# A graph network's kernel: sixteen rows a step fetched by SyncE, and the two convolutions' ends rearranged

## The chip, the cores and the metric

The kernel runs on one core of a Trainium2 chip. Its engines each follow an instruction stream of their own and wait for one another through semaphores: PE (TensorE) multiplies matrices, DVE (VectorE) does elementwise work and reductions, ACT (ScalarE) does functions such as silu and sqrt, POOL (GpSimd) here issues the gathers of rows, and SP (SyncE) issues all other transfers. The metric is the device time of one execution in microseconds (us).

## The reference

A block of a graph network on N = 6,250 nodes with 128 features and 200,000 edges, which are sorted by their destination. Two mesh convolutions and one attention stage, each over all edges:

```python
h = relu(layernorm(x))
# mesh_conv, twice
m = concat([h[dst], h[src], edge_attr]) @ w1 + b1
m = silu(group_norm(m)) @ w2 + b2
h = segment_sum(m, dst) / max(count, 1)      # then group_norm, silu, and + time embedding / + x
# attention
logits = (q[dst] * k[src]).sum(-1) * scale + (edge_attr @ ew + eb)
w = segment_softmax(logits, dst)
o = segment_sum(w * v[src], dst) @ ow + ob
x = x + (h + group_norm(o))
```

The two halves of each `concat` are products per node, so they are made once per node and kept in tables in the chip's main memory: `a_d` (what an edge takes from its destination) and `b_d` (what it takes from its source); for attention `kv_d` holds k and v in rows of 256 numbers.

## The kernel before

**Tiles, chunks, windows.** The edges are cut into 1,563 tiles of 128, one edge per partition, and the tiles into 196 chunks of 8 (TPC; the last has 3). The nodes are cut into 49 windows of 128. A stage (conv 1, conv 2, attention as stage 3) walks over its chunks in `pipeline`, one step for each; the order of the instructions on DVE, ACT, PE and SP within a step is written out there and kept.

**A chunk of a convolution.** SP loads the destination rows `pk` (L724) and, every second step, numbers for the one-hot matrices `ohT` (L708, L711). POOL gathers the source rows into `g`, one instruction for each tile (L767), into a ring of buffers ahead of the use. ACT turns `ohT` into one-hot form (L733, L734). PE multiplies `ohT` with `pk` (L1227). DVE adds the product to `g` (L1234, "first"); ACT squares (L1236), DVE reduces (L1238), ACT takes the root (L1245), DVE the reciprocal, and three DVE operations of the whole chunk normalise (`normed`, L1249 to L1253). ACT applies silu (L1254), PE sums by destination (`summed`, L1259), ACT splits the sums by window (`by_window`, L1264) and DVE adds them to the nodes (`add_late`, L1269).

**Rows by SP.** For every eleventh chunk ("lone" chunks, 17 in a stage) POOL gathers only seven tiles. The eighth is fetched by SP, which loads twelve row numbers into its registers in each step (L689), works out an address for each, and issues a transfer of one row into `row_g` (L693); after eleven steps the 128 rows are there, and ACT copies them into `g` (L700). The class `Rows` does this; `by_rows` lists the chunks.

**Node work.** Once the edges of four windows are all summed, their node work is done beside the chunks, a piece in each step: a *batch* (`conv_nodes`, L1008 to L1074), whose products give the next stage's tables and whose copies (`n_o`, L1067, or additions L1065) are then stored. `plan_batches` lists the steps at which batches start: 14 in a convolution, at 81, 89 and so on to 185. A batch waits some idle steps before its silu (`n_t`, L966), the last one none. The nine windows that remain are done after the pipeline by `last_nodes`, with the tiles of its own pool. Before it every engine passes a barrier.

**Between the stages.** `last_nodes` stores the last rows of the tables, and the next stage's first gather waits for these stores. In the memory on the chip the tiles of `last_nodes` after conv 2 lie where stage 3 has its buffers `g`.

The functions that the change touches:

Of the kernel before, what the change touches and what calls it, by code (L numbers as in the profile page):

```python
# [10 lines left out]
I32 = mybir.dt.int32  # L11
AF = mybir.ActivationFunctionType
# [19 lines left out]
BN = 4  # L32
LG = 2
# [4 lines left out]
ROWS = 12  # L38
# [13 lines left out]
def kernel(ctx: ExitStack, tc: tile.TileContext, x, src, dst, eat, w, out):  # L52
# [607 lines left out]
    class Rows:  # L660


        def __init__(self, pool, table_d, width):
            self.pool, self.table_d, self.width = pool, table_d, width
            self.chunks, self.span = by_rows()
            self.starts = {c - 2 - self.span: c for c in self.chunks}
            self.now, self.got = None, {}
            self.at = {}
            if self.chunks:
                self.list_of(self.chunks[0])  # L670

        def list_of(self, c):
# [3 lines left out]
            self.at[c] = t  # L676

        def step(self, n):
            if n in self.starts:
# [6 lines left out]
            if self.now:  # L686
# [3 lines left out]
                    self.at[c][0:1, e:e + m], engines=[SP], min_val=0, max_val=N - 1,  # L690
                    skip_runtime_bounds_check_because="a source node")
                for j, a in enumerate(at):
                    nc.sync.dma_start(out=t[e + j:e + j + 1, :], in_=self.table_d[bass.ds(a, 1), :self.width])  # L693
# [252 lines left out]
    class Nodes:  # L946
# [14 lines left out]
        def turned(self, t, m, tag="x", silu=None):  # L961
# [3 lines left out]
            if silu:  # L965
                nc.scalar.activation(out, tp, AF.Silu, bias=cols[f"{silu}_b"], scale=cols[f"{silu}_g"])  # L966
            else:
                nc.scalar.copy(out, tp)
# [33 lines left out]
    def conv_nodes(b, i, w, m, idle=0, last=False):  # L1002
# [26 lines left out]
        if i == 1 or last:  # L1029
# [5 lines left out]
            tT = b.turned(A, m, "t", silu=f"n{i}")  # L1035
# [21 lines left out]
        for rhs, bias, d_ in ends:  # L1057
            o = b.times(tT, m, rhs)
            if bias:
# [97 lines left out]
    def last_nodes(i, hx=True):  # L1157

        with tc.tile_pool(name="lastn", bufs=1) as lp, tc.tile_pool(name="lastp", bufs=6, space=PSUM) as ps:
# [28 lines left out]
    def conv(i):  # L1188
# [6 lines left out]
        with ExitStack() as es:  # L1195
# [52 lines left out]
            def normed(k):  # L1248
                nc.vector.tensor_tensor(  # L1249
                    k.mt.rearrange("p t (g c) -> p t g c", c=HD), k.mt.rearrange("p t (g c) -> p t g c", c=HD),  # L1250
                    k.rs.rearrange("p (t g) -> p t g", g=H)[:, :, :, None].to_broadcast([P, k.nt, H, HD]), ALU.mult)
                nc.vector.tensor_tensor(k.mt, k.mt, over_edges(gam, k.nt), ALU.mult)  # L1252
                nc.vector.tensor_tensor(k.mt, k.mt, over_edges(bet, k.nt), ALU.add)  # L1253
                nc.scalar.activation(k.mt, k.mt, AF.Silu)  # L1254
# [16 lines left out]
            class Stage:  # L1271
# [38 lines left out]
                def second(self, run, ks, first):  # L1310
# [3 lines left out]
                    for k in ks:  # L1314
# [3 lines left out]
                        if k.c >= NCH - SOON and self.sums:  # L1318
# [4 lines left out]
                        normed(k)  # L1323
# [33 lines left out]
            stage.rows = Rows(rw, b_d[i], D)  # L1357
# [46 lines left out]
    with ExitStack() as es:  # L1404
# [168 lines left out]
        class Stage:  # L1573
# [4 lines left out]
            def __init__(self, bp):  # L1578
                self.bp = bp
                self.rows = Rows(rw, kv_d, KV)  # L1580
# [200 lines left out]
```

## Time and profile before

| what | before |
|---|---|
| median of 3 runs | 6,077.24 us (6,076.54 to 6,078.74) |
| profiled execution, its own time | 6,073.33 us |
| profiled execution, span | 6,071.6 us |
| gathers, conv 1 | 1,546, first at 56.23 us, last ends at 1,995.11 |
| gathers, conv 2 | 1,546, first at 2,059.76 us, last ends at 3,995.26 |
| gathers, stage 3 | 1,546, first at 4,049.09 us, the last near 5,991 |
| busy share of the span | DVE 82%, POOL 73%, PE 59%, PEld 56%, ACT 55% |

The span is what the profiler recorded of one execution. A row of a timeline reads: start, duration, engine, line of the kernel, operation, output and input tiles, and in brackets the idle time of the engine before it and what ended it. A row of groups gives busy time and mean duration in ns after the bar, and the idle time before with its releaser after the second bar. An engine with a q (SPq) is that engine's instruction queue, which issues transfers.

### The profile page before, as it was taken

The numbers are of one execution on the slowest core, as the hardware profiler recorded it, in microseconds if no ns is written. First come the engines' busy times: TensorE is split into PE (matmuls) and PEld (weight loads), VectorE is DVE, ScalarE is ACT, GpSimd is POOL, SyncE is SP. The second block draws the span as 40 slices with busy tenths as digits, with TensorE's granted clock in tenths as the row PEclk, the third lists the DMA queues.
The fourth block names the chain that finished last, engine by engine and source line by source line (L and its number), as shares of the span: only waits on it lengthen the run. The fifth ranks groups of instructions, "written<-read, shape, count | busy, mean of one in ns | idle before, by whom it ended". The sixth has DMA issues, their size and how long they took to land. (4 is left out here: it accounts for less than half of the span.)

```text
span 6071.6 us, 88562 instructions
## 1 busy us (share of the span) xinstructions
PE 3607.7 (59%) x20941; PEld 3418.2 (56%) x20942; DVE 4995.9 (82%) x7118; ACT 3351.4 (55%) x5310; POOL 4446.9 (73%) x4687
## 2 busy tenths in 40 slices
PE   5565556556556555555666666655666665566665
PEld 4555555555556455555555655554555555565554
DVE  7888888888888588878888888865788888888888
ACT  5666666666666566666666666642333333333354
POOL 5777777777777477777777777757777777777775
PEclk8777777777777677777778777776777777777787
DMA  5454343444444343443444444435566666656663
GB/s 159 116 133 120 100 112 101 109 109 104 109 104 111 75 103 97 102 103 100 104 114 115 110 115 111 116 104 155 159 162 165 167 165 166 168 159 168 164 166 85
DMA packets 409874, 760.21 MB, mean 125 GB/s; under 512 B 102703, under 2 KB 276530, under 8 KB 379937
## 3 DMA queue, kind: packets, MB, share of 16 engines
q0 software_dynamic: 173152, 405.57, 26.4%
q1 hardware_dynamic: 230544, 345.24, 21.0%
q10 hardware_dynamic: 5632, 3.50, 0.2%
q8 instruction: 173, 2.83, 0.2%
q14 instruction: 373, 3.06, 0.2%
HBM read 707.36 MB, written 46.58 MB: 124 GB/s over the span
## 5 line engine op out<-in xcount | busy, mean ns | idle before, releaser
L767 POOL DMA_INDIRECT g<-b_d,src_i x3092 | 2931.6, 948 | 954.3 <-issue 904.4
L1259 PE MATMUL u<-h,oh 128*128 128x129 f32 (+1 forms) x6252 | 1265.1, 384 | 1388.4 <-ACT h L1254 1388.2
L1259 PEld LDWEIGHTS u<-h,oh 128*128 128x128 f32 x6252 | 1167.1, 288 | 1469.8 <-ACT h L1254 1465.4
L767 POOL DMA_INDIRECT g<-kv_d,src_i x1546 | 1470.0, 951 | 490.6 <-issue 439.8
L1227 PE MATMUL m<-pk,ohT 101*128 101x128 f32 x6252 | 961.7, 319 | 193.1 <-DVE h L1234 151.7
L1227 PEld LDWEIGHTS m<-pk,ohT 101*128 101x128 f32 x6252 | 932.7, 236 | 210.3 <-DVE h L1234 166.9
L1234 DVE TENSOR_TENSOR h<-m,g 128x1024 f32<-128x1024 f32 x392 | 475.8, 1214 | 477.4 <-DMA g<-b_d,src_i 462.8
L1518 PE MATMUL us<-v,oh 128*128 128x145 f32 x3126 | 590.3, 357 | 378.3 <-DVE flat L1543 329.3
L1518 PEld LDWEIGHTS us<-v,oh 128*128 128x128 f32 x3126 | 545.2, 248 | 418.1 <-DVE flat L1543 241.8
L1438 PE MATMUL qe<-pk,ohT 101*128 101x136 f32 x3126 | 558.1, 348 | 335.0 <-ACT ebs L1455 319.1
L1438 PEld LDWEIGHTS qe<-pk,ohT 101*128 101x128 f32 x3126 | 518.6, 249 | 367.6 <-ACT ebs L1455 360.8
L1254 ACT ACTIVATE h<-h 128x1024 f32<-128x1024 f32 x392 | 412.9, 1053 | 544.5 <-DVE h L1253 527.9
L1236 ACT ACTIVATE sq<-h 128x1024 f32<-128x1024 f32 x392 | 411.8, 1051 | 486.3 <-DVE h L1234 484.1
L733 ACT ACTIVATE ohT<-ohT,minus_p 96x1024 f32<-96x1024 f32 x588 | 669.3, 1138 | 19.6 <-DMA ohT<-rel_d 19.5
L734 ACT ACTIVATE ohT<-ohT 96x1024 f32<-96x1024 f32 x588 | 619.9, 1054 | 18.7
L1238 DVE TENSOR_REDUCE var<-sq 128x64 f32<-128x1024 f32 x392 | 475.0, 1212 | 105.8 <-ACT sq L1236 105.0
L1252 DVE TENSOR_TENSOR h<-h,cps 128x1024 f32<-128x1024 f32 x392 | 477.1, 1217 | 13.5
L1253 DVE TENSOR_TENSOR h<-h,cps 128x1024 f32<-128x1024 f32 x392 | 477.0, 1217 | 13.4
L790 DVE TENSOR_TENSOR oh<-cps,dm 128x1024 f32<-128x1024 f32 x392 | 474.1, 1209 | 2.1 <-PE u L1259 2.1
L1249 DVE TENSOR_TENSOR h<-h,cps 128x1024 f32<-128x1024 f32 x392 | 473.9, 1209 | 0.0
L1453 DVE TENSOR_TENSOR g<-qe,g 128x768 f32<-128x768 f32 (+1 forms) x391 | 251.2, 683 | 211.2 <-DMA g<-kv_d,src_i 203.9
L1531 ACT ACTIVATE us<-d 128x16 f32<-128x16 f32 x196 | 36.6, 187 | 638.2 <-DVE d L1527 566.3
(288 smaller groups left out, 4271.9 us busy)
## 6 DMA issues: line engine op xcount, KB each, us to landing
ohT<-rel_d SPq DMA_DIRECT2D x291, 768.0 KB
row_g<-b_d SPq DMA_DIRECT2D x4352, 0.5 KB
g<-b_d,src_i POOLq DMA_INDIRECT x3092
row_g<-kv_d SPq DMA_DIRECT2D x2176, 1.0 KB
pk<-a_d SPq DMA_DIRECT2D x588, 46.0 KB
g<-kv_d,src_i POOLq DMA_INDIRECT x1546, 3.1
ohT<-in_eat_dram SPq DMA_DIRECT2D x291, 40.0 KB
a_d<-n_o SPq DMA_DIRECT2D x28, 256.0 KB
```

Of the source, the lines that this page charges most:

```text
L733: nc.scalar.activation(k.ohT[:WN, :], k.ohT[:WN, :], AF.Square, bias=minus_p[:WN])
L734: nc.scalar.activation(k.ohT[:WN, :], k.ohT[:WN, :], AF.Relu, bias=1.0, scale=-4.0)
L767: h = nc.gpsimd.indirect_dma_start(out=g[:, t, :table_d.shape[1]], out_offset=None, in_=table_d, in_offset=bass.IndirectOffsetOnAxis(ap=k. ...
L790: return nc.vector.tensor_tensor(k.oh[:, :k.nt, :], iota[:, None, :].to_broadcast([P, k.nt, P]), k.dm[:, :, None].to_broadcast([P, k.nt, P ...
L1227: nc.tensor.matmul(k.m[:, t, :], lhsT=lhs[:, t * P:(t + 1) * P], rhs=rhs, start=(j == 0), stop=(j == len(terms) - 1))
L1234: nc.vector.tensor_tensor(k.mt, k.m[:, :n], k.g[:, :n], ALU.add)
L1238: return lambda: nc.vector.tensor_reduce(var[:, at:at + n * H], sq[:, :n].rearrange("p t (g c) -> p (t g) c", c=HD), AX.X, ALU.add)
L1252: nc.vector.tensor_tensor(k.mt, k.mt, over_edges(gam, k.nt), ALU.mult)
L1253: nc.vector.tensor_tensor(k.mt, k.mt, over_edges(bet, k.nt), ALU.add)
L1259: nc.tensor.matmul(k.u[:, 0, :wide], lhsT=k.oh[:, t, :], rhs=k.h[:, t, :wide], start=(t == 0), stop=(t == k.nt - 1))
L1438: nc.tensor.matmul(k.qe[:, t // TB, at:at + DB], lhsT=lhs[:, t * P:(t + 1) * P], rhs=rhs, start=(j == 0), stop=(j == len(terms) - 1))
L1518: nc.tensor.matmul(k.u[:, :wide], lhsT=k.oh[:, t, :], rhs=k.v[:, t, :wide], start=(t == 0), stop=(t == k.nt - 1))
```

## The change

**Rows.** `ROWS` becomes 16: eight steps for a tile, every eighth chunk, 23 lone chunks in a stage instead of 17, at 13, 21 and so on to 189. DVE multiplies each list of row numbers by the row's length in bytes (`to_bytes`, 69 small instructions in the three stages, four steps after the list is requested). The table is seen as one run of bytes, so SP uses the number as an address. Fifteen of a step's sixteen transfers count up one of two semaphores of their own; only the sixteenth is tracked by the framework. ACT's copy waits for the count.

On SP, a step with rows in conv 1 before (`pk` is the load of destination rows, `row_at` the list of numbers); the pair of rows at the end goes on to twelve:

```order
L724 ISA
L724 DMA pk_662<-a_d_95 92x128
L689 TENSOR_LOAD row_at
L693 ISA
L693 DMA row_g<-b_d_98 1x128
```

and after:

```order
L748 ISA
L748 DMA pk_661<-a_d_95 92x128
L702 TENSOR_LOAD row_at
L708 DMA row_g<-b_d_98 1x512 x16
L748 ISA
L748 DMA pk_662<-a_d_95 92x128
L732 DMA ohT<-rel_d 96x2048
L735 DMA ohT<-in_eat_dram 5x2048
```

The arithmetic (ISA) ahead of each row is gone, and sixteen transfers stand in one run. POOL issues 1,540 gathers in each stage instead of 1,546.

**Batches of the convolutions.** They start at steps with remainder 5 by 8, at 85, 93 and so on to 181, and none in the last ten steps: 13 instead of 14. In conv 1 the last three have no idle steps, and with `fine` the last two spread a batch's transposes, silu, products and copies over more steps.

On ACT in conv 1, from the square of chunk 190 (`sq<-h_701`) on. Before, with a batch's copy (`n_o`), another's silu (`n_t`) and its table load ahead of the next compare (`ohT`):

```order
L1236 ACTIVATE sq<-h_701 128x1024
L1245 ACT_TABLE_LOAD
L1245 ACTIVATE sd<-var,eps_t 128x64
L1067 COPY n_o<-nd 128x512
L966 ACT_TABLE_LOAD
L966 ACTIVATE n_t<-nd,k_n_b,k_n_g 128x512
L733 ACTIVATE ohT<-ohT,minus_p 96x1024 x2
L734 ACTIVATE ohT<-ohT 96x1024
```

After:

```order
L1269 ACTIVATE sq<-h_701 128x1024
L1278 ACT_TABLE_LOAD
L1278 ACTIVATE sd<-var,eps_t 128x64
L757 ACTIVATE ohT<-ohT,minus_p 96x1024
L758 ACTIVATE ohT<-ohT 96x1024
L1301 ACTIVATE u<-u,mask 128x129 x2
L1291 ACT_TABLE_LOAD
L1291 ACTIVATE h_701<-h_701 128x8x128
L1269 ACTIVATE sq<-h_702 128x1024
L1278 ACT_TABLE_LOAD
L1278 ACTIVATE sd<-var,eps_t 128x64
L1096 COPY n_o<-nd 128x512
```

The last batch's silu now stands at step 188, one copy at step 190 ahead of these rows and the other at step 192, the last row shown. In conv 2 the last batch ends within the pipeline; before, its last addition (L1065, q) stood behind the pipeline's last sums.

**The last full chunk.** Chunk 194 is normalised in two halves of four tiles, and its sums are split by window only behind those of chunk 195. The last rows of ACT in a convolution's pipeline, before:

```order
L1264 ACTIVATE u<-u,mask 128x129 x2
L1254 ACT_TABLE_LOAD
L1254 ACTIVATE h_701<-h_701 128x8x128
L1264 ACTIVATE u<-u,mask 128x129 x2
L1254 ACTIVATE h_702<-h_702 128x3x128
```

and after:

```order
L1301 ACTIVATE u<-u,mask 128x129 x2
L1291 ACT_TABLE_LOAD
L1291 ACTIVATE h_701<-h_701 128x4x128 x2
L1291 ACTIVATE h_702<-h_702 128x3x128
L1301 ACTIVATE u<-u,mask 128x129 x4
```

The silu of chunk 194 became two, and the splits moved behind the silu of chunk 195.

**Between conv 2 and stage 3.** An unused tile of 50,528 bytes a partition ("below") moves the tiles of `last_nodes` up. They no longer lie under stage 3's `g`, but under its buffers `nbs`, `nbe`, `row_at` and the second `ohT`. The first gather of stage 3 waited for all eight lanes of SP's transfers before (stores of `kv_d`, `a_d` and `h_d`), and for six after (those of `kv_d`). On SP the loads of `row_at`, `nbs`, `nbe` and the first `ohT` now stand behind the `h_d` stores; before, they stood in conv 1's end.

The diff, at its core:

```diff
-ROWS = 12
+ROWS = 16
+BELOW = 12632
@@ plan_batches
-            if n % 8 == (4 if i == 3 else 1) and n > (40 if i == 3 else 80) and n + 6 < NCH \
+            if n % 8 == (4 if i == 3 else 5) and n > (40 if i == 3 else 80) and n + (6 if i == 3 else 10) < NCH \
@@ class Rows
+            self.bytes_d = table_d.rearrange("n c -> (n c)").bitcast(U8)
+            self.landed = [[tc.alloc_semaphore(f"{name}{j}"), 0] for j in range(2)]
+        def to_bytes(self, t):
+            nc.vector.tensor_scalar(t, t, 4 * self.width, None, ALU.mult)
         def step(self, n):
+            self.fresh -= 1
+            if self.fresh == 0:
+                self.to_bytes(self.at[max(self.at)])
...
                 for j, a in enumerate(at):
-                    nc.sync.dma_start(out=t[e + j:e + j + 1, :], in_=self.table_d[bass.ds(a, 1), :self.width])
+                    h = nc.sync.dma_start(out=t[e + j:e + j + 1, :].bitcast(U8),
+                                          in_=self.bytes_d[bass.ds(a, 4 * self.width)][None, :])
+                    if j == m - 1:
+                        tc.declare_fence(h.ins, group=key)
+                        continue
+                    tc.no_tile_sem_insts.add(h.ins.name)
+                    h.then_inc(s[0], 16)
+                    s[1] += 16
+                    tc.add_to_no_dep_group(key, h.ins)
...
-                nc.scalar.copy(k.g[:, TPC - 1, :self.width], self.got.pop(k.c))
+                s = self.landed[self.chunks.index(k.c) % 2]
+                nc.scalar.copy(k.g[:, TPC - 1, :self.width], self.got.pop(k.c)).wait_op(s[0], s[1], "sem-ge")
@@ conv_nodes
-            tT = b.turned(A, m, "t", silu=f"n{i}")
+            tp = b.in_bank(A, m)
+            if fine > 0:
+                yield
+            tT = b.silu_of(tp, m, f"n{i}")
...
-            if bias:
+            if bias or fine > 1:
                 yield
@@ last_nodes
+            if i == 2:
+                es.enter_context(tc.tile_pool(name="below", bufs=1)).tile([P, BELOW], FP, name="below")
@@ normed
-            def normed(k):
+            def normed(k, by=TPC):
+                for a in range(0, k.nt, by):
@@ second
-                        if k.c >= NCH - SOON and self.sums:
+                        if NCH - SOON <= k.c < NCH - 1 and self.sums:
...
-                        normed(k)
+                        normed(k, TPC // 2 if k.c == NCH - 2 else TPC)
@@ batch
-                    for r in conv_nodes(nodes, i, w, BN, idle=4 if j + 1 < len(plans[i]) else 0):
+                    for r in conv_nodes(nodes, i, w, BN, idle=4 if j + (3 if i == 1 else 1) < len(plans[i]) else 0,
+                                        fine=(j + 3 - len(plans[i])) * (i == 1)):
```

More of the change, by code (lines that the diff above doesn't have):

```diff
@@ L11 @@
 I32 = mybir.dt.int32
+U8 = mybir.dt.uint8
 AF = mybir.ActivationFunctionType
@@ L660, with __init__ @@
     class Rows:
[L663 to L664 removed]
+        def __init__(self, pool, table_d, width, name):
+            self.pool, self.table_d, self.width, self.name = pool, table_d, width, name
+            self.bytes_d = table_d.rearrange("n c -> (n c)").bitcast(U8)
             self.chunks, self.span = by_rows()
+            self.landed = [[tc.alloc_semaphore(f"{name}{j}"), 0] for j in range(2)]
             self.starts = {c - 2 - self.span: c for c in self.chunks}
@@ L670, in __init__ @@
                 self.list_of(self.chunks[0])
+                self.to_bytes(self.at[self.chunks[0]])
+                self.fresh = 0
         def list_of(self, c):
@@ L689, in step @@
                 _, at = nc.values_load_multi_w_load_instructions(
-                    self.at[c][0:1, e:e + m], engines=[SP], min_val=0, max_val=N - 1,
-                    skip_runtime_bounds_check_because="a source node")
+                    self.at[c][0:1, e:e + m], engines=[SP], min_val=0, max_val=(N - 1) * 4 * self.width,
+                    skip_runtime_bounds_check_because="where a source node's row begins")
+                s = self.landed[self.chunks.index(c) % 2]
+                key = f"{self.name}_{c}_{e}"
                 for j, a in enumerate(at):
-                    nc.sync.dma_start(out=t[e + j:e + j + 1, :], in_=self.table_d[bass.ds(a, 1), :self.width])
+                    h = nc.sync.dma_start(out=t[e + j:e + j + 1, :].bitcast(U8),
[7 more added lines that the diff above has]
+                    tc.add_to_no_dep_group(key, h.ins)
                 self.now[1] = e + m
@@ L959, in in_bank, with turned, silu_of @@
             return tp[:, :m, :]
-        def turned(self, t, m, tag="x", silu=None):
+        def turned(self, t, m, tag="x"):
             tp = self.in_bank(t, m)
             out = self.tile(m, tag)
[L965 to L968, printed above, removed]
+            nc.scalar.copy(out, tp)
+            return out
+        def silu_of(self, tp, m, n):
+            out = self.tile(m, "t")
+            nc.scalar.activation(out, tp, AF.Silu, bias=cols[f"{n}_b"], scale=cols[f"{n}_g"])
             return out
@@ L1000, in span, with conv_nodes @@
         return bass.ds(w, m) if not isinstance(w, int) else slice(w, w + m)
-    def conv_nodes(b, i, w, m, idle=0, last=False):
+    def conv_nodes(b, i, w, m, idle=0, last=False, fine=0):
         at = span(w, m)
@@ L1157, in last_nodes @@
     def last_nodes(i, hx=True):
-        with tc.tile_pool(name="lastn", bufs=1) as lp, tc.tile_pool(name="lastp", bufs=6, space=PSUM) as ps:
+        with ExitStack() as es:
+            if i == 2:
+                es.enter_context(tc.tile_pool(name="below", bufs=1)).tile([P, BELOW], FP, name="below")
+            lp = es.enter_context(tc.tile_pool(name="lastn", bufs=1))
+            ps = es.enter_context(tc.tile_pool(name="lastp", bufs=6, space=PSUM))
             n = NW - NWD
@@ L1246, in deviations @@
                 return sd
-            def normed(k):
[L1249 to L1254, printed above, removed]
+            def normed(k, by=TPC):
+                for a in range(0, k.nt, by):
+                    n = min(by, k.nt - a)
+                    mt = k.mt[:, a:a + n]
+                    m4 = mt.rearrange("p t (g c) -> p t g c", c=HD)
+                    nc.vector.tensor_tensor(
+                        m4, m4, k.rs.rearrange("p (t g) -> p t g", g=H)[:, a:a + n, :, None].to_broadcast(
+                            [P, n, H, HD]), ALU.mult)
+                    nc.vector.tensor_tensor(mt, mt, over_edges(gam, n), ALU.mult)
+                    nc.vector.tensor_tensor(mt, mt, over_edges(bet, n), ALU.add)
+                    nc.scalar.activation(mt, mt, AF.Silu)
             def summed(k):
@@ L1356, in conv @@
             stage = Stage()
-            stage.rows = Rows(rw, b_d[i], D)
+            stage.rows = Rows(rw, b_d[i], D, f"rows{i}")
             nodes.var = lambda: stage.var[:, NV:]
@@ L1579, in __init__ @@
                 self.bp = bp
-                self.rows = Rows(rw, kv_d, KV)
+                self.rows = Rows(rw, kv_d, KV, "rows3")
                 self.runs = list(steps_of(3)[0].values())
```

1 line of the change is left out of this document (added).

## The prediction

> **What bounds the kernel now.** I read the costliest groups first, then the waits, then the busy time of each stage's stretch of gathers, and last the timelines around the ends of the two convolutions. The page's chain of waits holds only shares of 0% and says nothing here.
>
> ```profile
> L767 POOL DMA_INDIRECT g<-b_d,src_i x3092 | 2931.6, 948 | 954.3 <-issue 904.4
> ...
> L767 POOL DMA_INDIRECT g<-kv_d,src_i x1546 | 1470.0, 951 | 490.6 <-issue 439.8
> ```
>
> ```profile
> POOL g L767 <- issue: 1344.2, 4409, 0.3
> ...
> DVE h L1234 <- DMA g<-b_d,src_i: 462.8, 166, 15.0
> ```
>
> ```profile
> core 0: us, PE busy (x) PEld busy (x) DVE busy (x) ACT busy (x) POOL busy (x), PEclk, DMA share, GB/s
> 56.00:1996.00 1940.00, 1144.99 (x6728) 1095.99 (x6726) 1610.21 (x1787) 1262.20 (x1558) 1467.15 (x1546) 0.75 0.44 112
> 2059.00:3996.00 1937.00, 1157.35 (x6756) 1105.44 (x6757) 1619.74 (x1663) 1251.99 (x1535) 1464.44 (x1546) 0.75 0.42 108
> 4049.00:5991.00 1942.00, 1184.46 (x6748) 1104.76 (x6748) 1594.07 (x3305) 740.91 (x2019) 1469.99 (x1546) 0.76 0.61 163
> ```
>
> Each stage issues 1,546 gathers. One keeps POOL busy 0.948 us and the next follows 0.30 us later, released by nothing but its own issue: a pitch of 1.25 us, 1,546 of which are the 1,937 to 1,942 us of each stretch. DVE is busy longer than POOL (1,610 us) but idles 17%, and in the convolutions its largest wait is for a gather. So POOL's sequence of gathers sets the pace, and the three stretches make 5,819 of the 6,071.6 us. The remainder lies around the stages' ends. At conv 1's end DVE's first operation on each of chunks 189 to 195 (L1234) stands so, with POOL's last gather ahead of it:
>
> ```profile
> 1994.17 0.94 POOL L767 DMA_INDIRECT g<-b_d,src_i  x1 [0.30 <-issue]
> ```
>
> ```profile
> 1947.07 1.22 DVE L1234 TENSOR_TENSOR h<-m,g 128x1024 f32<-128x1024 f32 x1
> ...
> 1966.48 1.22 DVE L1234 TENSOR_TENSOR h<-m,g 128x1024 f32<-128x1024 f32 x1
> ...
> 1977.63 1.22 DVE L1234 TENSOR_TENSOR h<-m,g 128x1024 f32<-128x1024 f32 x1
> ...
> 1993.19 1.22 DVE L1234 TENSOR_TENSOR h<-m,g 128x1024 f32<-128x1024 f32 x1
> ...
> 2005.23 1.22 DVE L1234 TENSOR_TENSOR h<-m,g 128x1024 f32<-128x1024 f32 x1
> ...
> 2017.63 1.22 DVE L1234 TENSOR_TENSOR h<-m,g 128x1024 f32<-128x1024 f32 x1
> ...
> 2021.11 0.55 DVE L1234 TENSOR_TENSOR h<-m,g 128x384 f32<-128x384 f32 x1
> ```
>
> The last gather ends at 1995.11 and the last chunk begins at 2021.11: DVE is 26.0 us behind. Chunk 189 was not: 42 gathers of 1.249 us follow its own (chunk 192 has 7, chunk 195 has 3), so its last ended at about 1942.65 and L1234 came 4.4 us later. The steps from chunk 189 to 194 took 19.4, 11.2, 15.6, 12.0 and 12.4 us, 70.6 in all, where their 39 gathers took 48.7. What makes them long is the node work of two batches, both still unfinished there. ACT, which goes strictly in order, stands 5.18 us before a batch's copy, and all later compares and square roots stand behind it:
>
> ```profile
> 2005.95 0.58 ACT L1067 COPY n_o<-nd 128x512 f32<-128x512 f32 x1 [5.18 <-PE nd L974]
> ```
>
> Conv 2, with one batch unfinished, loses less; the same rows for chunks 189, 190 and 192 to 195:
>
> ```profile
> 3994.32 0.94 POOL L767 DMA_INDIRECT g<-b_d,src_i  x1 [0.30 <-issue]
> ```
>
> ```profile
> 3943.98 1.23 DVE L1234 TENSOR_TENSOR h<-m,g 128x1024 f32<-128x1024 f32 x1
> ...
> 3961.70 1.22 DVE L1234 TENSOR_TENSOR h<-m,g 128x1024 f32<-128x1024 f32 x1
> ...
> 3981.30 1.22 DVE L1234 TENSOR_TENSOR h<-m,g 128x1024 f32<-128x1024 f32 x1
> ...
> 3989.79 1.22 DVE L1234 TENSOR_TENSOR h<-m,g 128x1024 f32<-128x1024 f32 x1
> ...
> 3998.53 1.22 DVE L1234 TENSOR_TENSOR h<-m,g 128x1024 f32<-128x1024 f32 x1
> ...
> 4002.60 0.55 DVE L1234 TENSOR_TENSOR h<-m,g 128x384 f32<-128x384 f32 x1
> ```
>
> One step of 17.7 us (the batch's silu), then undisturbed ones of 8.5 to 8.7: DVE catches up 1.3 us a chunk and ends 7.3 us behind the gather that ended at 3995.26.
>
> **Part 1, more rows by SP.** Six gathers fewer in each of three stages are 18 x 1.249 = **22.5 us**, if POOL still sets the pace. In stage 3 the last chunks run DVE-bound, but before and after alike two lone chunks lie there, so all six count. What it costs falls on SP, the DMA engines and DVE. SP's rows in one step before, in a convolution and in stage 3, and what one DMA and one load of row numbers take:
>
> ```profile
> 1015.24 5.12 SPq L693 DMA_DIRECT2D row_g<-b_d  x12
> ```
>
> ```profile
> 4910.59 7.84 SPq L693 DMA_DIRECT2D row_g<-kv_d  x12
> ...
> 4921.06 4.80 SPq L693 DMA_DIRECT2D row_g<-kv_d  x12
> ```
>
> ```profile
> L693 SPq DMA_DIRECT2D row_g<-b_d x4352: 224/228/1167, 95.1 to 3941.2; - x198
> ```
>
> ```profile
> L689 SPq TENSOR_LOAD <-row_at x561: 687/1007/2876, 93.9 to 5947.2; - x187
> ```
>
> Unhindered, twelve rows take 4.80 us, 0.40 each, of which the DMA is 0.228; the arithmetic between them goes. Sixteen then cost between 16 x 0.228 = 3.6 and 16 x 0.40 = 6.4 us. I take 0.30 a row, 4.8 us, nearer the lower end since the instruction that goes is the larger part of the difference. With 1.0 for the numbers' load and about 1.1 for the step's pk and ohT loads a step costs SP some 7 us (5.7 to 8.5), against 1,540 / 196 x 1.249 = 9.81 us of gathers. So it is hidden behind POOL, and only a row over (9.81 - 2.1) / 16 = 0.48 us would come through. The 7.84 us above shows that rows can be hindered (0.65 each): there a row waits for a semaphore lane that another load holds, and fifteen of sixteen rows no longer use one.
>
> The 2,304 rows more (69 x 128 less 51 x 128) load the DMA engines:
>
> ```profile
> q1 hardware_dynamic: 230544, 345.24, 21.0%
> ```
>
> 21.0% of 16 engines over 6,071.6 us, by 230,544 packets, is 0.0885 us a packet. The page counts 102,703 packets under 512 B, close to 6,528 rows x 16. So 36,864 more are 204 us for each of 16 engines, 3.4% of the span; the busiest stretch stands at 0.61 and goes to about 0.64. I count nothing, and at the other end 3.4% of stage 3's gathers' landing, which its 11 buffers cover. The Trainium skill speaks against it: "DMA: Bandwidth & Descriptors", section Specifications, wants at least 512 B for the line rate, and its section on semaphore increments splits one transfer over up to 16 engines. The trace agrees on the splitting; by that rule the rows are the dearest way to move these bytes, yet the sum stays, since engine time isn't what is short.
>
> The 69 multiplications of row numbers are small DVE instructions, priced by the nearest row:
>
> ```profile
> 2040.21 0.17 DVE L1008 TENSOR_SCALAR n_c<-flat 128x3 f32<-128x3 f32 x1 [2.33 <-DMA wcl<-wc_d]
> ```
>
> 69 x 0.17 = 12 us, 4 in each stage, inside DVE's 330 us of idleness in each: nothing, at most 12 if none were covered. The Trainium skill's "SBUF — State Buffer", section Who interferes with whom, has a tensor_scalar able to take the port that GpSimd shares, the other one blocking for the whole instruction. By that rule the sum would lose up to those same 12 us; the trace's gathers keep their 0.30 us gaps beside a DVE that is 83% busy.
>
> **Part 2, the batches earlier.** Conv 1's last two batches start at steps 173 and 181, not 177 and 185, and without idle steps; the earlier one is out of the tail, and the last has its silu at step 188 and two copies at 190 and 192. I charge the silu half of conv 2's excess of 7.7 us (its transposes are a step earlier now), each copy's step 2.2 us over ten (the 12.0 and 12.4 above), and give back 1.3 for each of three undisturbed ones: 4.4 + 3.9 + 4.4 - 3.9 = 8.8 us behind at the end, so 26.0 - 8.8 = **17 us**. Bounds: 21.6 if the tail ends as chunk 189 stood (4.4 behind), and 10 with both copies as dear as the 15.6 step. In conv 2 the silu also comes earlier: 2 us off the 7.3, between 0 and 4.
>
> **Part 3, the ends.** After the last chunk's first operation comes a fixed chain, up to the first gather of the next stage:
>
> ```profile
> 2037.45 0.42 DVE L1269 TENSOR_TENSOR flat<-flat,u 128x258 f32 x1 [2.48 <-ACT u L1264]
> ```
>
> ```profile
> 4018.34 0.68 DVE L1065 TENSOR_TENSOR n_o<-nd,r_qb 128x512 f32<-128x512 f32 x1
> 4022.72 0.31 DVE L1013 COPY n_c<-cnt 128x6 f32<-128x6 f32 x3 [3.70 <-SPq L799]
> ```
>
> ```profile
> L1015 DVE TENSOR_TENSOR n_x<-flat,n_c 128x512 f32<-128x512 f32 x28 | 19.4, 693 | 0.5
> ```
>
> Chunk 194 in halves starts its silu after three operations of 0.69 instead of 1.22 us, so 1.6 earlier, and products of chunk 195 and the window sums no longer wait in turn: about **3 us** of the 16.8 from 2021.11 to 2037.87 (between 0 and 4). Conv 2 has the same 3, and its last batch no longer runs past the pipeline: no addition at 4018.34 (0.7) and a barrier that need not wait for the batch's last store (3.70 against conv 1's 2.33, 1.3): **5 us**, between 2 and 6.
>
> ```profile
> 4036.95 4.94 SPq L1062 DMA_DIRECT2D kv_d<-n_o  x6
> ...
> 4044.01 1.80 SPq L1074 DMA_DIRECT2D h_d<-n_x  x3
> ```
>
> ```profile
> 4049.09 0.95 POOL L767 DMA_INDIRECT g<-kv_d,src_i  x1 [18.81 <-DMA ohT<-in_eat_dram]
> ```
>
> With the padded tile, stage 3's first gather waits for six lanes, those of the kv_d stores, not for eight. Their issue ends at 4041.89, the h_d stores' at 4045.81, 3.9 us later, and the gather started 3.3 after that. So **4 us**, 0 to 5. In exchange the nbs, nbe and first ohT loads are issued behind the h_d stores, on SP; chunk 0's compare is then late by a few us, with 11 chunks' worth of gather buffers to absorb it.
>
> Sum: 22.5 + 17 + 2 + 3 + 5 + 4 = **53.5 us**. The profiled execution took 6,073.33 by its own time, span 6,071.6 and 1.7 around it; that less 53.5 is 6,019.8. The median of the runs shown is 3.9 above the profiled one, so **6,024 us**.
>
> **Rivals.** *The tail stays long* (0.18): the copies wait for products that PE does in its own order, as the 5.18 us row shows, and two of them remain, so conv 1's steps stay near 12 to 15 us. Then its 17 and conv 2's 2 shrink to 3: 37.5 saved, 6,040. Against it: conv 2's undisturbed steps of 8.5. *Only the gathers count* (0.09): the ends turn out to be bound by PE's sums or by landing stores, and 22.5 is all: 6,055. *The rows take the gain back* (0.05): the 3.4% more engine time holds up the gathers' own transfers until POOL's gaps grow. A pitch of 1.258 instead of 1.249 (0.7%, a fifth of 3.4) on 4,620 gathers is 42 us: 6,066, within 0.2%. For: the gathers use the same 16 engines. Against: stage 3 at a share of 0.61 has the pitch of the convolutions at 0.44. *SP becomes the pace* (0.05, the other side): at L693 of the kernel before, the rows of one step. For: 7.84 us for twelve. From 0.48 us a row, SP's step is longer than the gathers', the copy out of row_g comes late, and POOL runs out of free g buffers. Each 0.01 us above costs 16 x 0.01 x 552 steps (23 chunks x 8 x 3) = 88 us; at 0.50 it is 177 less the 53 gained, 6,200. Against: unhindered it is 0.40 with the arithmetic that goes.
>
> **How the numbers follow.** The forecast has 0.63 and its own range 6,014 (every part at its better end, 63 us) to 6,036 (41 us; all at the worse end, 34.5, is less likely). The tail rival takes the range to 6,040, and 6,048 with some of the ends' terms lost besides; below it goes to 6,011, by the 2.2 us that the runs shown spread over. 6,011 to 6,048 leaves out the last three rivals. A change under 0.2% (12 us) can't be told from none here. Faster: 0.63 + 0.18 + 0.09 = 0.90; same 0.05; slower 0.05.
>
> **What would show it.** Right: 1,540 gathers a stage at an unchanged pitch of 1.25 us; row fetches x16 in about 5 us; L1234 of conv 1's chunk 195 about 9 us behind the last gather; 35.7 us rather than 38.7 from there to the next stage's first gather, and 37.5 rather than 46.5 at conv 2's end. Wrong: a row above 0.48 us, POOL waiting for a buffer, conv 1's steps after chunk 189 still 12 us or more, or gather gaps above 0.30 us beside the multiplications.

## The result, and the profile after

The changed kernel took a median of 6,022.5 us (four runs, 6,018.4 to 6,025.0) against 6,078.0 for the kernel before beside it; the ratio is 0.9907, with a 95% interval of 0.9890 to 0.9924. The forecast was 6,024 and its range 6,011 to 6,048. The profiled execution has a span of 6,016.3 us, 55.3 less than before. One set of the experiments ran on a chip on which SP was held up, where the kernel before took 8,584 us; it is compared with that time alone.

The groups and waits that answer to those shown of before, of the changed kernel (a gather is L791 now, DVE's first operation on a chunk L1267):

```profile
L791 POOL DMA_INDIRECT g<-b_d,src_i x3080 | 2921.7, 949 | 950.9 <-issue 903.8
...
L791 POOL DMA_INDIRECT g<-kv_d,src_i x1540 | 1464.4, 951 | 484.8 <-issue 433.4
```

```profile
POOL g L791 <- issue: 1337.2, 4386, 0.3
...
DVE h L1267 <- DMA g<-b_d,src_i: 444.4, 157, 14.7
```

POOL still waits for nothing but its own issue: 0.949 us and 0.30 behind it, as before, now 1,540 times a stage. Busy time in the three stretches of gathers:

```profile
56.00:1989.00 1933.00, 1128.99 (x6759) 1080.38 (x6757) 1623.85 (x1814) 1273.80 (x1574) 1462.52 (x1540) 0.76 0.44 112
2029.00:3957.00 1928.00, 1138.42 (x6736) 1086.18 (x6736) 1620.87 (x1675) 1253.55 (x1539) 1458.77 (x1540) 0.75 0.43 108
4000.00:5934.00 1934.00, 1169.24 (x6734) 1089.78 (x6735) 1598.53 (x3330) 745.61 (x2023) 1463.94 (x1540) 0.77 0.63 165
```

Conv 1's end, first POOL's last gather, then DVE's timeline: the first operations of chunks 189 to 195, DVE's last sum, and the first operation of the last nodes. The last row's bracket is the idle time before it:

```profile
1987.94 0.95 POOL L791 DMA_INDIRECT g<-b_d,src_i  x1 [0.30 <-issue]
```

```profile
1939.21 1.22 DVE L1267 TENSOR_TENSOR h<-m,g 128x1024 f32<-128x1024 f32 x1
...
1953.21 1.22 DVE L1267 TENSOR_TENSOR h<-m,g 128x1024 f32<-128x1024 f32 x1
...
1962.41 1.22 DVE L1267 TENSOR_TENSOR h<-m,g 128x1024 f32<-128x1024 f32 x1
...
1970.84 1.22 DVE L1267 TENSOR_TENSOR h<-m,g 128x1024 f32<-128x1024 f32 x1
...
1979.27 1.22 DVE L1267 TENSOR_TENSOR h<-m,g 128x1024 f32<-128x1024 f32 x1
...
1987.70 1.22 DVE L1267 TENSOR_TENSOR h<-m,g 128x1024 f32<-128x1024 f32 x1
...
1991.18 0.56 DVE L1267 TENSOR_TENSOR h<-m,g 128x384 f32<-128x384 f32 x1
...
2004.36 0.42 DVE L1306 TENSOR_TENSOR flat<-flat,u 128x258 f32 x1 [1.01 <-ACT u L1301]
...
2009.52 0.17 DVE L1034 TENSOR_SCALAR n_c<-flat 128x3 f32<-128x3 f32 x1 [4.73 <-issue]
```

The last gather ends at 1988.89 and chunk 195 begins 2.3 us later, where it was 26.0. One step, from chunk 189 to 190, still takes 14.0 us; the others take 8.4 to 9.2, and those of 8.4 catch up 1.5 us a chunk. The copies no longer make ACT wait; in the long step it waits for PE's sums:

```profile
1943.14 0.56 ACT L1096 COPY n_o<-nd 128x512 f32<-128x512 f32 x1
...
1953.17 0.72 ACT L1301 ACTIVATE u<-u,mask 128x129 f32<-128x129 f32 x2 [3.90 <-PE u L1296]
...
1966.29 0.57 ACT L1096 COPY n_o<-nd 128x512 f32<-128x512 f32 x1
```

That wait does not set the step's length. DVE is busy for 13.5 of the 14.0 us (the third pair of numbers below), for it normalises two chunks in this step (L1286 to L1290 run twice between two rows of L1267):

```profile
1939.21:1953.21 14.00, 7.64 (x48) 7.16 (x48) 13.49 (x16) 9.32 (x12) 10.60 (x12) 0.76 0.41 115
```

Conv 2's end on DVE (chunk 195's first operation, the last sum, the first operation of the last nodes), then POOL's last gather of conv 2 and stage 3's first:

```profile
3960.16 0.56 DVE L1267 TENSOR_TENSOR h<-m,g 128x384 f32<-128x384 f32 x1 [1.20 <-DMA g<-b_d,src_i]
...
3972.45 0.42 DVE L1306 TENSOR_TENSOR flat<-flat,u 128x256 f32 x1 [0.47 <-ACT u L1301]
3977.77 0.32 DVE L1039 COPY n_c<-cnt 128x6 f32<-128x6 f32 x3 [4.89 <-issue]
```

```profile
3956.51 0.94 POOL L791 DMA_INDIRECT g<-b_d,src_i  x1 [0.30 <-issue]
...
4000.39 0.95 POOL L791 DMA_INDIRECT g<-kv_d,src_i  x1 [15.08 <-ACT n_x L989]
```

Cut at these rows, the two profiled executions compare like this:

| piece of the span, us | before | after | saved |
|---|---|---|---|
| three stretches of gathers | 5,816.2 | 5,795.1 | 21.1 |
| conv 1: last gather's end to chunk 195's first operation | 26.0 | 2.3 | 23.7 |
| conv 1: from there to DVE's last sum | 16.8 | 13.6 | 3.2 |
| conv 1: from there to the last nodes' first operation | 2.3 | 4.7 | -2.4 |
| conv 2: last gather's end to chunk 195's first operation | 7.3 | 2.7 | 4.6 |
| conv 2: from there to DVE's last operation | 16.4 | 12.7 | 3.7 |
| conv 2: from there to the last nodes' first operation | 3.7 | 4.9 | -1.2 |
| conv 2: from there to stage 3's first gather | 26.4 | 22.6 | 3.8 |
| behind stage 3's last gather | 80.7 | 81.9 | -1.2 |

Together they are 55.3 us, with conv 1's last nodes at 19.5 us both times.

### The profile page after: what moved, and what is told of

Same layout as the page of the kernel before. It is cut to its first block, busy times and chain, and to the rows that moved or that the text cites. A ratio compares the mean times of both kernels' runs of the same rounds, so it can differ in the third digit from the quotient of the medians.

```text
span 6016.3 us, 86748 instructions
## 1 busy us (share of the span) xinstructions
PE 3547.9 (59%) x20869; PEld 3359.6 (56%) x20870; DVE 4994.1 (83%) x7165; ACT 3355.0 (56%) x5321; POOL 4431.3 (74%) x4669
## 3 DMA queue, kind: packets, MB, share of 16 engines
q1 hardware_dynamic: 234576, 345.26, 21.4%
## 5 line engine op out<-in xcount | busy, mean ns | idle before, releaser
L791 POOL DMA_INDIRECT g<-b_d,src_i x3080 | 2921.7, 949 | 950.9 <-issue 903.8
L1296 PE MATMUL u<-h,oh 128*128 128x129 f32 (+1 forms) x6252 | 1250.0, 381 | 1400.3 <-ACT h L1291 1400.2
L1296 PEld LDWEIGHTS u<-h,oh 128*128 128x128 f32 x6252 | 1153.9, 285 | 1481.1 <-ACT h L1291 1475.7
L791 POOL DMA_INDIRECT g<-kv_d,src_i x1540 | 1464.4, 951 | 484.8 <-issue 433.4
L1260 PE MATMUL m<-pk,ohT 101*128 101x128 f32 x6252 | 933.8, 313 | 179.4 <-DVE h L1267 134.0
L1260 PEld LDWEIGHTS m<-pk,ohT 101*128 101x128 f32 x6252 | 902.7, 229 | 197.2 <-DVE h L1267 150.2
L1267 DVE TENSOR_TENSOR h<-m,g 128x1024 f32<-128x1024 f32 x392 | 475.8, 1214 | 463.0 <-DMA g<-b_d,src_i 444.4
L1291 ACT ACTIVATE h<-h 128x1024 f32<-128x1024 f32 (+2 forms) x394 | 413.5, 1049 | 571.0 <-DVE h L1290 554.9
L1289 DVE TENSOR_TENSOR h<-h,cps 128x1024 f32<-128x1024 f32 (+2 forms) x394 | 477.5, 1212 | 13.5
L1290 DVE TENSOR_TENSOR h<-h,cps 128x1024 f32<-128x1024 f32 (+2 forms) x394 | 477.4, 1212 | 13.5
L1286 DVE TENSOR_TENSOR h<-h,cps 128x1024 f32<-128x1024 f32 (+2 forms) x394 | 474.1, 1203 | 0.0
```

Source lines behind the costliest of these rows:

```text
L791: h = nc.gpsimd.indirect_dma_start(out=g[:, t, :table_d.shape[1]], out_offset=None, in_=table_d, in_offset=bass.IndirectOffsetOnAxis(ap=k. ...
L1260: nc.tensor.matmul(k.m[:, t, :], lhsT=lhs[:, t * P:(t + 1) * P], rhs=rhs, start=(j == 0), stop=(j == len(terms) - 1))
L1267: nc.vector.tensor_tensor(k.mt, k.m[:, :n], k.g[:, :n], ALU.add)
L1289: nc.vector.tensor_tensor(mt, mt, over_edges(gam, n), ALU.mult)
L1290: nc.vector.tensor_tensor(mt, mt, over_edges(bet, n), ALU.add)
L1296: nc.tensor.matmul(k.u[:, 0, :wide], lhsT=k.oh[:, t, :], rhs=k.h[:, t, :wide], start=(t == 0), stop=(t == k.nt - 1))
```

## Experiments

Theory: POOL's gathers set the pace, SP's longer steps are hidden, and the batches' unfinished work was what made conv 1's tail long. Rivals: SP is near its limit; the tail had another cause; the rows and the ends don't add up.

**The rows alone, and the ends alone.**

```diff
# e1_rows_only: the kernel before with class Rows and its calls as changed
-ROWS = 12
+ROWS = 16
# e2_ends_only: the changed kernel with class Rows and its calls as before
-ROWS = 16
+ROWS = 12
```

> The kernel before with the rows' part alone: sixteen rows a step, byte addresses, own semaphores; batches, last chunk and memory of the ends as before. Theory (POOL's gathers set the pace, SP's longer steps are hidden): 18 gathers fewer, which the profile of after shows as 6 to 8 us in each stage, 21 in all, so about 6,057 us; conv 1's last chunk still begins 20 us or more behind its last gather. Rival (the rows by themselves cost what they save, and the ends made the whole gain): within 6 us of 6,078.

Measured: 6,057.4 us, ratio 0.9969 (0.9957 to 0.9980). Conv 1's lag stayed at 26.0 us, conv 2's at 7.3; the stretches of gathers were 1,933.0, 1,931.9 and 1,934.6 us.

> The changed kernel with the rows as before: twelve a step, SP's register arithmetic, tracked one by one, 1,546 gathers a stage; batches, halves and the tile below as changed. Theory (the parts add up): 6,022 plus the 21 us of 18 gathers, about 6,043; conv 1's last chunk begins 2 to 6 us behind its last gather, as in after. Rival (the short tail needs the rows' part, since before a lone chunk lay at 192 and SP was busier): a lag of 10 us or more in conv 1, and 6,052 or above.

Measured: 6,038.8 us, ratio 0.9939 (0.9923 to 0.9956), lags of 2.1 and 2.7 us. Against their runs of the kernel before (6,075.7) the rows save 18 us (12 to 26 by the interval) and the ends 37 (27 to 47), together 55, as the whole change does: as far as these intervals tell they add up, and neither needs the other.

**The batches as before.**

```diff
-            if n % 8 == (4 if i == 3 else 5) and ... and n + (6 if i == 3 else 10) < NCH \
+            if n % 8 == (4 if i == 3 else 1) and ... and n + 6 < NCH \
-                    for r in conv_nodes(..., idle=4 if j + (3 if i == 1 else 1) < len(plans[i]) else 0, fine=...):
+                    for r in conv_nodes(..., idle=4 if j + 1 < len(plans[i]) else 0):
```

> The changed kernel with the batches of the convolutions as before (14, at steps 81 to 185, idle steps in all but the last, none of the finer pieces); rows, halves and the tile below as changed. Theory (the batches' unfinished work makes the tail long): conv 1's last chunk begins 20 to 26 us behind its last gather and conv 2's 7, so some 21 + 4 us more than the changed kernel, about 6,048. Rival (the tail was long for another reason, such as the lone chunk at 192 or the last chunks' order): conv 1's lag stays under 10 us and the time within 6 of 6,022.

Measured: 6,044.5 us, 22 more than the changed kernel. Conv 1's lag is 19.3 us, just short of the 20 to 26 expected, conv 2's 7.3, and the copies wait again:

```profile
1951.05 0.59 ACT L1096 COPY n_o<-nd 128x512 f32<-128x512 f32 x1 [4.16 <-PE nd L1000]
...
1968.67 0.59 ACT L1096 COPY n_o<-nd 128x512 f32<-128x512 f32 x1 [3.74 <-PE nd L1000]
...
1981.83 0.59 ACT L1096 COPY n_o<-nd 128x512 f32<-128x512 f32 x1 [4.19 <-PE nd L1000]
...
1994.87 0.59 ACT L1096 COPY n_o<-nd 128x512 f32<-128x512 f32 x1 [4.75 <-PE nd L1000]
```

So the old batches are the cause of the long tail: with the same rows and halves, four copies fall into the tail and wait some 4 us each, 16.8 together, where the changed kernel has two copies that don't wait and a lag 17.0 us shorter. The run undoes the starts, the idle steps and the finer pieces together. That the finer pieces end the waits, because products that come a step after the silu are ready as ACT reaches the copy, is argued, not shown. Nor do the runs say what took the other 6.7 of conv 1's 23.7 us, for the rows alone left the lag at 26.0.

**The halves and the tile below, undone.**

```diff
-                        if NCH - SOON <= k.c < NCH - 1 and self.sums:
+                        if k.c >= NCH - SOON and self.sums:
-                        normed(k, TPC // 2 if k.c == NCH - 2 else TPC)
+                        normed(k)
-            if i == 2:
-                es.enter_context(tc.tile_pool(name="below", bufs=1)).tile([P, BELOW], FP, name="below")
```

> The changed kernel with two parts of the ends undone: chunk 194 normalised in one piece with its sums split where they were, and no tile that moves the last nodes' memory up before stage 3. Each is read at its own place in the trace. Theory: from the last chunk's first operation to DVE's last sum 16.8 and 16.4 us, as in the kernel before, not 13.6 and 12.7; and from the last nodes' first operation in conv 2 to stage 3's first gather 26.4, not 22.6 us. Some 10 us more than the changed kernel in all, less what the wait at the branch of L823 changes by. Rival for the tile below (the kv_d stores land last anyway, and the other stores cost nothing): 22.6 stays. Rival for the halves (the short tail of the batches alone brought the 3 us): 13.6 and 12.7 stay.

Measured, one run: 6,039.2 us, 17 more than the changed kernel where some 10 were expected. From chunk 195's first operation to DVE's last sum 16.8 us in conv 1 and 15.8 in conv 2 (16.4 before included a batch's addition); from the last nodes' first operation in conv 2 (3989.84) to stage 3's first gather 26.4 us:

```profile
4016.26 0.95 POOL L791 DMA_INDIRECT g<-kv_d,src_i  x1 [18.86 <-DMA pk<-a_d]
```

So both parts do what the forecast said: 3 us at each convolution's end, 3.8 before stage 3. Conv 1's lag was 6.4 us here, 4.1 more than with the halves. It opens at chunk 191, which neither part touches, where ACT waited for a load of `ohT` that came late:

```profile
1953.33 1.15 ACT L757 ACTIVATE ohT<-ohT,minus_p 96x1024 f32<-96x1024 f32 x1 [4.30 <-DMA ohT<-rel_d]
```

The changed kernel's profile has no such wait there; one run doesn't tell how often it comes.

**SP's budget: sixteen rows in the old way.**

```diff
 # the kernel before
-ROWS = 12
+ROWS = 16
```

> The kernel before with ROWS = 16 and nothing else: sixteen rows a step with SP's register arithmetic and with every row waiting for a lane. Theory of SP's pace: a row costs a mean of 0.50 us this way (5.8 us for twelve in the trace of before), so a step costs SP 16 x 0.50 + 1.2 + 1.1 = 10.3 us against 9.81 of gathers; 0.5 us more on some 184 steps in each stage, 270 us, less the 21 gained: about 6,330, and POOL waits for free buffers. Rival (the lane waits only fill SP's slack, and a row costs 0.40 where it matters): 8.7 us a step, hidden, 6,057 as with the byte addresses.

Measured: 6,424.1 us, ratio 1.0576 (1.0558 to 1.0594). This is the prediction's rival on the slower side, and it is what the rows would have cost without the byte addresses and own semaphores. A row cost 0.47 to 0.49 us on average. SP's waits for a free `ohT` buffer, which are its slack, show it best; before, after, and here:

```profile
SPq L708 <- PE m L1227: 526.1, 135, 12.9
...
SPq L708 <- PE qe L1438: 251.7, 50, 13.9
```

```profile
SPq L732 <- PE m L1260: 619.9, 160, 10.0
SPq L732 <- PE qe L1476: 366.3, 70, 17.2
```

```profile
SPq L708 <- PE m L1227: 47.8, 8, 13.2
SPq L708 <- PE qe L1438: 45.8, 4, 15.9
```

778 us of slack before, 986 after (with more rows), 94 here. With it gone ACT waits for loads (the wait of the first row below was 19.5 us before), and POOL for the chunks that should free its buffers:

```profile
ACT ohT L733 <- DMA ohT<-rel_d: 900.9, 186, 12.1
```

```profile
POOL g L767 <- DVE h L1234: 164.5, 91, 7.6
POOL g L767 <- DVE n_rs L1142: 162.4, 17, 11.2
```

The forecast for this run was 6,330, with 10.3 us a step; conv 1 took 2,043.5 us, 10.4 for each of its 196 chunks. Sixteen rows at 0.47 and 1.4 from the list's load to the first row leave about 1.4 us for the rest of a step, an estimate, where 1.1 was counted.

**Bytes, but every row tracked.** Here on an undisturbed chip; the same kernel on the other one is under "More rows".

```diff
-                    if j == m - 1:
-                        tc.declare_fence(h.ins, group=key)
-                        continue
-                    tc.no_tile_sem_insts.add(h.ins.name)
-                    h.then_inc(s[0], 16)
-                    s[1] += 16
-                    tc.add_to_no_dep_group(key, h.ins)
```

> The changed kernel with byte addresses but every row tracked, so that each of the sixteen waits for one of the eight lanes as before. Theory (of the 0.50 us a row before, 0.09 are lane waits: 588 us of them on 6,528 rows, and 0.08 the register arithmetic): 0.41 a row, 1.4 + 16 x 0.41 + 1.4 = 9.4 us a step, just hidden: 6,020 to 6,040. Rival (the lanes alone bring SP to its limit): 0.45 or more a row, a step above 9.9 us, 6,080 or more, with POOL waiting for buffers.

Measured: 6,043.8 us (two runs), ratio 0.9944 (0.9924 to 0.9964), 4 us above the range expected, with 0.41 us a row in conv 1 and 0.44 in stage 3. The convolutions' gathers are within 3 us of the changed kernel's (1,932.1 and 1,931.4 us), but stage 3's take 1,945.8 instead of 1,934.1 and its end 91.0 instead of 81.9. So of the old 0.50 us a row, 0.09 were arithmetic and 0.08 lane waits, and without the own semaphores SP's slack is down to 293 us:

```profile
SPq L705 <- DMA ohT<-rel_d: 603.0, 276, 4.6
SPq L721 <- PE m L1249: 229.7, 76, 10.7
...
SPq L721 <- PE qe L1465: 63.5, 9, 17.2
```

The first row is what rows waited for lanes; in the changed kernel it is gone. Roughly 20 us of the change's gain hang on the semaphores.

**More rows.** Four kernels ran on the chip with the held-up SP, whose single instructions were up to 1.4 us long there (source lines of `e9_shift88`; minimum, median and maximum in ns):

```profile
L708 SPq MOVE row_g<-b_d x5888: 1/29/1437, 121.3 to 5287.6; - x197
L708 SPq DMA_DIRECT2D row_g<-b_d x5888: 1/228/1424, 121.3 to 5287.6; - x197
```

Only places that SP doesn't reach are read from them.

```diff
-ROWS = 16
+ROWS = 19      # rows19; rows22: 22
```

> The changed kernel with ROWS = 19: seven steps for a tile, every seventh chunk, 27 lone chunks in a stage, four gathers fewer in each stage than the changed kernel. Theory (POOL's pace; SP's step of 1.4 for the list + 19 x 0.326 + 1.4 for the rest = 9.0 us stays under the 9.78 of the gathers): 12 gathers at the 1.16 us that each of the 18 brought so far, 14 us, about 6,008. Rival (the gain by gathers is used up, DVE or the batches set the pace from here): 6,018 to 6,026, and DVE no longer waits for gathers.

> The changed kernel with ROWS = 22: six steps for a tile, 31 lone chunks in a stage, eight gathers fewer in each. Theory of SP's pace: a step costs SP 1.4 + 22 x 0.326 + 1.4 = 10.0 us against 9.76 of gathers, so SP sets the pace by 0.2 us a step, some 45 us in each stage less 10 for the gathers: 6,100 or more, with ACT or PE waiting for loads and POOL for buffers. Rival (the other 1.4 us overlap or are rarer; SP stays hidden): 24 gathers x 1.16 = 28 us less than the changed kernel, 5,995.

> The changed kernel with byte addresses but every row tracked, so that each of the sixteen waits for one of the eight lanes as before. Theory (of the 0.50 us a row before, 0.09 were lane waits and 0.08 the register arithmetic): 0.41 a row, 16 x 0.41 + 2.8 = 9.4 us a step, just hidden: 6,020 to 6,035. Rival (the lanes are the larger part of what the change saves on SP): 0.45 or more a row, a step above 9.9 us, 6,100 or more.

Measured: ratios 1.1198 (1.1161 to 1.1236), 1.1771 (1.1741 to 1.1802) and 1.0022 (1.0001 to 1.0043). With SP as the bound, more rows simply cost more; the expectations, made for an undisturbed SP, can't be judged by these. So nineteen rows were repeated, with the 88 memsets of the next experiment:

> The changed kernel with ROWS = 19 (27 lone chunks in a stage, 12 gathers fewer in all) and the 88 memsets in conv 1 that move DVE's code. Theory: where SP is undisturbed a step costs it 1.4 + 19 x 0.326 + 1.4 = 9.0 us against 9.78 of gathers, so 12 x 1.16 = 14 us are gained; and the wait at the branch of L823 behind conv 1 is 0.5, not 2.9 us, likewise behind conv 2 if the place of the code decides it there too: 5 us; about 6,003 in all. Rival for the rows (SP is at its limit already): 6,030 or more, and POOL waits for buffers. Rival for the branch: 2.9 and 3.1 us stay, and the time is 6,008.

Measured: 6,617.5 us, ratio 1.0889 (1.0871 to 1.0907), where 6,003 was expected. The rows cost 0.326 us each, as in the changed kernel. SP's slack is down to 39 us, and POOL waits 497 us for chunks that should free its buffers. What I had not counted is the load of the row numbers (minimum, median and maximum in ns; first the changed kernel, then nineteen rows):

```profile
L702 SPq TENSOR_LOAD <-row_at x552: 1132/1234/3569, 93.2 to 5858.3; - x184
```

```profile
L702 SPq TENSOR_LOAD <-row_at x567: 1773/4099/6484, 93.9 to 6527.9; - x189
```

By the place of the step in the tile, medians from the same trace:

```
first number      0     19    38    57    76    95    114
numbers           19    19    19    19    19    19    14
load, us          2.05  4.14  4.14  4.13  1.86  4.14  3.14
```

Where the first number divides by 4, nineteen numbers take half as long. Steps of twelve and of sixteen always begin so. The last experiment uses that: steps of 20 and 16 rows in turn begin at 0, 20, 36, 56, 72, 92 and 108.

```diff
-ROWS = 16
+ROWS = 20
-                m = min(ROWS, P - e)
+                m = ROWS if e % (ROWS + 16) == 0 else 16
```

> The changed kernel with steps of 20 and 16 rows in turn (seven steps for a tile, 27 lone chunks, 12 gathers fewer in all), every step beginning at a row number that divides by 4, and with the 88 memsets in conv 1. Nineteen rows a step made SP's loads of the row numbers take 4.1 us where the first number did not divide by 4, and 1.8 to 2.1 where it did. Theory (that load made SP the pace, not the rows themselves): loads of about 1.9 and 1.3 us, a step of 1.6 + 18.3 x 0.326 + 1.4 = 9.0 us on average against 9.78 of gathers, hidden; 14 us by gathers and 2.4 at the branch behind conv 1: about 6,006. Rival (more than 16 rows a step cost too much in any case): 6,030 or more, with POOL waiting for buffers.

Measured: 6,014.2 us (6,008.0 to 6,016.6), ratio 0.9892 (0.9876 to 0.9909); the loads' median is 1.44 us and POOL waits for no buffer. It is 8 us below the changed kernel's median, but the two intervals overlap, and each is measured against its own runs of the kernel before; so it is at best slightly faster. Of 12 gathers fewer, conv 1's stretch shows 2.4 us, conv 2's 4.5 and stage 3's none (1,935.6 against 1,934.1), and conv 2's lag is 9.1 instead of 2.7. SP's slack is 477 us. The load was what made SP the pace, since seven steps fetch the 128 rows in both kernels. But the steps of 20 and 16 differ from those of nineteen in two things, in where they begin and in a count that divides by 4. Both seem to matter: from a place that divides by 4, 20 numbers took 1.46 us and 19 took 1.86. The 14 us don't stand: stage 3's end no longer follows the number of gathers.

**DVE's wait at the branch.** Behind conv 1's last sum DVE reaches the branch of L823, and in the changed kernel its next instruction comes 2.9 us later, before 0.5 (this is the -2.4 of the table). It is no wait for another engine: ACT, POOL and SP were past the same branch by 2005.3 us, and the semaphores that DVE's next instruction asks for had been raised at 1992.8, while that instruction came at 2008.1.

```diff
+            spare = rw.tile([1, 8], FP, name="spare") if i == 1 else None
                 def reduce(self, k):
                     k.reduce()
+                    if i == 1 and 40 <= k.c < 128:
+                        nc.vector.memset(spare, 0.0)
```

> The changed kernel with 88 one-partition memsets added on DVE in conv 1, one in each of 88 chunks: they do no work that is used and only move DVE's later instructions. In the trace of the changed kernel DVE stands 2.9 us at the branch of L823 behind conv 1's last chunk, in that of the kernel before 0.5 us. Theory (the place of the code behind the branch decides it, by when instructions are fetched): with 88 instructions more the 2.9 us become about 0.5, and conv 2 begins 2.4 us earlier, with 88 x 0.06 us = 5 us hidden in DVE's idle time. Rival (what runs before the branch, the short tail itself, decides it): the wait stays at 2.9 +- 0.3.

Measured on the disturbed chip, but DVE's instructions were undisturbed there: 0.54 us (ratio of the whole to the kernel before 0.9874, 0.9841 to 0.9906). On an undisturbed chip the two later kernels with the memsets agree, here `e10_rows20_16`, with 2.36 us idle instead of 4.73:

```profile
2005.45 0.17 DVE L1034 TENSOR_SCALAR n_c<-flat 128x3 f32<-128x3 f32 x1 [2.36 <-DMA wcl<-wc_d]
```

In conv 1, over all fourteen kernels, the wait goes with the number of DVE's instructions up to that branch: 2,515 to 2,530 and 2,650 to 2,659 gave 0.5 us, 2,560 to 2,581 gave 2.9 to 3.4. Behind conv 2, 4,887 and 4,977 to 5,033 gave 0.5, while 4,854, 4,940 to 4,957 and 5,045 gave 2.1 to 3.1, and behind stage 3 the wait was 2.7 to 3.1 in every kernel. So these runs give no rule for other places. Nor do the profile's loads of instructions settle the cause: in nine kernels on undisturbed chips two of 8,192 B begin 0.5 to 0.7 and 1.0 to 1.2 us behind conv 1's branch, whether the wait is the long or the short one. And the time won was partly lost again: in `e10_rows20_16` the last nodes took 21.3 us instead of 19.5.

## Why the prediction was right, point by point

**Gathers, 22.5 forecast, 21.1 measured.** POOL's pitch stayed, so 18 instructions fewer showed almost in full. Alone, the rows brought 18 us of time.

**SP's step, hidden.** Right, by a smaller margin than worked out. A row was put at 0.30 us and measured 0.326, the list's load at 1.0 and measured 1.24, the rest at 1.1 and came to about 1.4: 7.9 us a step instead of 7. The threshold of "0.48 us a row" was therefore mis-sized: (9.81 - 2.6) / 16 = 0.45. Rows at 0.47 already took 6,424 us, where the rival had 6,200 for rows at 0.50, and rows at 0.41 to 0.44 cost stage 3 some 20. The 0.40 of the old way was its best case, too: the mean over the kernel before is 0.50.

**The DMA engines' load, "204 us for each of 16 engines", was wrong.** I took 102,703 packets under 512 B for 6,528 rows in sixteen pieces and wrote that the trace agrees on the splitting; it does not. The changed kernel has 35% more rows and this:

```profile
DMA packets 413220, 758.53 MB, mean 126 GB/s; under 512 B 107215, under 2 KB 280274, under 8 KB 383297
...
q1 hardware_dynamic: 234576, 345.26, 21.4%
```

The queue has 4,032 packets more, not 36,864, and its share goes from 21.0 to 21.4% of a shorter span. With the rows alone (`e1_rows_only`) it has 7,200 more, and with the ends alone (`e2_ends_only`) 3,168 fewer. The 7,200 are two for each of the 2,304 rows, which leaves 144 for each of the 18 lists more. The trace's records of single packets show a row of a convolution as one of 512 B and one of 4 B behind it:

```
start us   ns  bytes
1009.568   25  512
1009.589    9  4
1010.261   27  512
1010.290    9  4
```

The packets under 512 B are such 4 B ones, and 74,208 of the 102,703 belong to the gathers. The Trainium skill's "DMA: Bandwidth & Descriptors", section "Why a DMA increments its semaphore by 16 and not by 1", takes the largest number up to 16 that divides the slowest dimension other than 1 of both sides, which I read as sixteen pieces for a row of 128 numbers or 512 bytes. The trace shows one piece, so the rule on transfers under 512 B had no weight here. The sum had counted it at nothing, for another reason: that it came out so is luck.

**The multiplications' 12 us.** Covered, as forecast: the gaps between gathers are still 0.30 us, and at most 0.31 beside the 69 multiplications. The possible port conflict named from the Trainium skill's "SBUF — State Buffer", section Who interferes with whom, did not show.

**Conv 1's tail, 17 forecast, 23.7 measured.** That the batches' unfinished work made it long was right, by the old batches' run, and so was the start: 4.4 us behind at chunk 189 forecast, 4.0 measured, worked out in the same way. The terms behind it failed. I charged 4.4 for two copies' steps, but neither copy made ACT wait for a product. I charged 3.9 for the silu, half of the excess of conv 2's step of 17.7 us, but DVE is busy for 14.1 us of that step, again with two chunks:

```profile
3943.98:3961.70 17.72, 9.50 (x62) 8.88 (x60) 14.12 (x16) 12.56 (x17) 13.45 (x15) 0.81 0.35 97
```

So more than half of that excess is DVE's own work, which stays whatever the batches do. In conv 1 it is the 4.0 us over ten of the step of 14.0 us; that this is close to the 3.9 is luck. The silu's own step (chunk 188, 11.5 us) ended with DVE waiting 2.5 us for a gather, so it cost nothing. The other steps gave back 5.5 us instead of 3.9. The sign of being wrong, "conv 1's steps after chunk 189 still 12 us or more", came true for that one step, and not by a batch. Conv 2's tail gave 4.6 instead of 2: its steps from chunk 189 on took 14.4, 8.6 and 8.5 us, where they had taken 17.7, 10.5 and 9.1.

**The ends, 3 + 5 forecast, 0.8 + 2.5 measured.** The step that failed is the barrier: DVE's part came 3.2 and 3.7 us sooner as worked out, but I let the branch behind it cost what it had cost before. It took 2.4 us more in conv 1, and in conv 2, where 1.3 was to be saved, 1.2 more.

**Stage 3's first gather, 4 forecast, 3.8 measured.** Shown by undoing the tile below. The loads that moved behind the `h_d` stores cost nothing visible.

Forecast 53.5, measured 55.3: the tails' extra 9 us covered what the gathers and the branch fell short, so that the sum came this close is partly luck.

## What to carry to other kernels

When one engine's queue of equal instructions sets the pace, every instruction taken off it is worth about its pitch (21 us for 18 here), as long as the engine that takes over has slack and nothing else becomes the pace: twelve more taken off, with steps of 20 and 16 rows, brought 7 us in the convolutions and nothing in stage 3. Read the slack from its waits for free buffers: of 778 us with twelve rows a step, sixteen rows at 0.47 us left 94, and the kernel was 5.8% slower. In an in-order queue, look for consumers that stand close behind their product: with the old batches such copies waited 4 us each, with the new ones not at all. Before a long step is put down to the work that was added to it, sum the busy time of the engine that paces it. At a stage's end, price the chain up to the next stage's first instruction piece by piece, branches among them.

## What the runs showed of the hardware that was not expected

- A load of row numbers into SP's registers took 1.0 us for 12 numbers, 1.23 for 16 and 1.46 for 20, with the first one's place and the count both divisible by 4. It took 1.86 us for 19 when only the place was, and 4.1 when neither was. These are medians; the first step of a tile took 0.2 more.
- Transfers of one row with an address from a register cost SP 0.326 us each, 0.41 with the waits for lanes, 0.50 with the arithmetic as well.
- The instruction behind a branch came 0.5 or about 3 us later, and 88 instructions more ahead of it moved it from the one to the other in conv 1. That this is when its code is fetched was argued, not shown.
